# Graph attention on one core: the masks of query blocks 2 and 3 made between the first graph's steps instead of ahead of them

## The chip, the cores and the metric

The kernel runs on one core of a Trainium2 chip. A core has TensorE (PE: matrix products, results in PSUM), VectorE (DVE), ScalarE (ACT), GpSimd (POOL) and SyncE (SP, which here only starts DMAs), each with its own instruction queue that it works off in order. The metric is the device time of one launch in microseconds. The three runs shown for the kernel before gave 3195.69, 3188.96 and 3193.34 us, median 3193.34 us.

## The reference

There are 8 graphs of 2048 nodes with 256 channels, and one adjacency matrix that all graphs share. Each graph goes through 8-head masked attention (32 channels a head) and a small feed-forward block, with three layer norms:

```python
q, k, v = jnp.split(jnp.einsum('fnc,ck->fnk', x, w_qkv), 3, axis=-1)      # then split into 8 heads of 32
scores = jnp.einsum('fnhd,fmhd->fhnm', q, k) / jnp.sqrt(D)
scores = jnp.where((adj > 0)[None, None], scores, -1e9)
t = jnp.einsum('fhnm,fmhd->fnhd', jax.nn.softmax(scores, -1), v).reshape(F, N, C)
x = _layernorm(x + t, ln1_g, ln1_b)
h = jax.nn.relu(jnp.einsum('fnc,cd->fnd', x, w1) + b1)
x = _layernorm(x + jnp.einsum('fnd,dc->fnc', h, w2) + b2, ln2_g, ln2_b)
...
return _layernorm(x_in + x)      # the layer's own input added, normalised once more
```

`adj` is a 2048x2048 int32 matrix. A node attends where `adj > 0`.

## The kernel before

**Steps.** The work is cut into items `(f, qc, g, mb)`: graph `f` (8), query block `qc` of 512 queries (4), head group `g` of four heads (2), key block `mb` of 128 keys (16). That is 1024 items, 128 for a graph (a *frame*), and one pass of the main loop (line 606) is one step `t`. For an item, `scores` (line 222) forms four 128x512 score blocks on PE, keys on the partitions, and DVE adds the mask to them on their way from PSUM to a `p` tile (line 233, two instructions of 128x1024). `exponentials` is one ACT instruction of 128x2048 (line 237). `values` multiplies by V on PE and accumulates over the 16 key blocks in one PSUM bank (line 249). `add_up` sums the exponentials for the softmax denominator: some key blocks are added by POOL (line 271), six of 16 by a DMA that adds 1 MB in SBUF and that POOL issues (line 268). Scores run two steps ahead (`LEAD = 2`) and share three PSUM pairs, two per step.

**Fill.** All other work is written as generators and put between the steps by `advance` (line 511), once per step: projections of the next graph's keys and values (`project`), queries (`ask`), turning the next graph's input (`turn`), denominators, normalisation and feed-forward (`tail`). A generator that yields `BANK` asks for the one PSUM bank that is left for fill, and gets it at most once per step, if the step's credit (`STEP = 2200`, and `UNIT = 1024` at least) allows it or its due time has come. A positive number means: wait so many steps. `INPUTS - 2` means: wait until the two oldest of the three input buffers are free. `NEXT` (line 553) says at which step of a frame each piece for the next graph starts; `start` takes the due time as its last argument.

**Turning the input.** `turn` (line 169) loads 512 rows of the next graph's `x`, waits five steps, transposes them on PE in two bank uses (`turn_rows`, line 161), and stores the result in device memory as `XD`. `reload` fetches it again for the projections.

**Masks.** DVE adds an fp8 value of 0 or -57344 to a score. The mask depends only on `(qc, mb)`, so it is made once for all graphs. `begin` (line 557) does it ahead of the main loop for all four query blocks: for each 512x512 piece of `adj` (16 pieces, 1 MB each, 2 KB runs) it loads a `p` tile, DVE compares and converts to bf16 in two instructions (line 582), `mask_blocks` (line 134) transposes 16 blocks of 128x128 on PE (line 141), two PSUM banks of eight, and evicts one through ACT (line 147) and one through DVE (line 145) as one byte per element. SP stores each 128 KB half in device memory as `MD[qc, k]` (line 148). During query blocks 0 and 1, `begin` also turns the first graph's input and projects its keys and values. After the last piece of query block 1 it issues the first two items' scores and the first exponential (lines 598 to 601), and then goes on with query blocks 2 and 3. In the main loop `load_mask` (lines 607 and 608) fetches `MD` for the next query block, one piece at every odd step of the second head group, into a ring of nine mask tiles.

**Buffers that the change touches.** Keys and values live in rings of 11 tiles of 2 KB per partition (`kp`, `vp`, lines 71 and 73). `work` holds one tile each of `turned` and `hT` (4 KB), used by the tail of a query block, `yp` two tiles `y` (4 KB). The first tail of graph 0 starts at step 47.

Of the kernel before, what the change touches and what calls it, by code (L numbers as in the profile page):

```python
# [10 lines left out]
F32 = mybir.dt.float32  # L11
BF16 = mybir.dt.bfloat16
I32 = mybir.dt.int32
I8 = mybir.dt.int8
F8 = mybir.dt.float8e5
AF = mybir.ActivationFunctionType
ALU = mybir.AluOpType
AX = mybir.AxisListType

P = 128  # L20
H = 8
D = 32
CH = 512
# [6 lines left out]
BANK, MORE, WAIT, TURNED, ROOM, INPUTS = -1, -2, -3, -4, -5, -10  # L30
STEP, UNIT, TURN, KEPT = 2200, 1024, 1400, 2200

MASKED = -57344.0
CODE = -5.0
# [27 lines left out]
def fast_path(ctx, tc, cst, x, adj, out, RS):  # L62
    nc = tc.nc
    F, N, C = x.shape
    NCK, TPC, MB = N // CH, CH // P, N // P
# [5 lines left out]
    kp = ctx.enter_context(tc.tile_pool(name="kp", bufs=3 * NCK - 1))  # L71
    qp = ctx.enter_context(tc.tile_pool(name="qp", bufs=4))
    vp = ctx.enter_context(tc.tile_pool(name="vp", bufs=3 * NCK - 1))
    pp = ctx.enter_context(tc.tile_pool(name="pp", bufs=12))
    work = ctx.enter_context(tc.tile_pool(name="work", bufs=1))
    yp = ctx.enter_context(tc.tile_pool(name="yp", bufs=2))
# [8 lines left out]
    ident, identb, wqkv, w1s, w2s = cst["ident"], cst["identb"], cst["wqkv"], cst["w1s"], cst["w2s"]  # L85
    state = {"pair": 0, "side": None, "turn": 0, "turned": False, "holder": None, "tails": 0, "credit": 0}
# [15 lines left out]
    def bank(dt=F32):  # L102
        shape = [P, CH] if dt == F32 else [P, 2, CH]
        if state["side"] is not None:
            i = 1 - state["side"]
            return ps_x[i].tile(shape, dt, name=f"x{i}")
        i = state["turn"]
        state["turn"] = (i + 1) % 5
        pool = ps_s[i] if i < 3 else ps_x[i - 3]
        return pool.tile(shape, dt, name=f"s{i}" if i < 3 else f"x{i - 3}")  # L110
# [11 lines left out]


    MD = dp.tile([NCK, MB // 2, P, 2 * CH // 4], I32, name="md")
    MK = {}

    def words(mask):
        return mask.rearrange("p b q -> p (b q)").bitcast(I32)
# [5 lines left out]
    def mask_blocks(qc, mc, cv, to=None):  # L134
        for half in range(2):
# [11 lines left out]
                nc.scalar.copy(m.bitcast(I8), ps)  # L147
            nc.sync.dma_start(MD[qc, k], words(m))

    def load_mask(f, qc, k):  # L150
        nc.sync.dma_start(words(mask_piece(f, qc, k)), MD[qc, k])

# [16 lines left out]
    def turn(f, c):  # L169
        yield INPUTS - 2  # L170
        xc, xT = take([P, TPC, C], F32), take([P, 2, CH], F32)
        nc.sync.dma_start(xc, x[f, c * CH:(c + 1) * CH, :].rearrange("(j p) c -> p j c", p=P))
        yield 5
        yield from turn_rows(xc, xT)
        give(xc)
        yield 1
        nc.sync.dma_start(XD[f][c], xT)
        XT[f, c] = xT
        give(xT)
# [315 lines left out]
    def start(t, gen, due):  # L495
        fill.append([t, gen, 1, due])
        fill.sort(key=lambda e: e[3])
# [13 lines left out]
    def advance(t, finish=False):  # L511
        state["credit"] = min(max(state["credit"], 0) + STEP, KEPT)
        state["now"] = t
        free = not state["holder"]

        def more():
            if state["holder"] and state["holder"][2] == WAIT:
                return False
            due = [e[3] for e in fill if e[2] == BANK and e[0] <= t or e is state["holder"]]
            return finish or state["credit"] >= UNIT or min(due) <= t  # L520

        if state["holder"]:
            resume(state["holder"], t)
            while state["holder"] and more():
                resume(state["holder"], t)
        inputs = True
        for e in list(fill):
            while e[2] is not None and e[0] <= t and e is not state["holder"]:
                if e[2] == BANK:
                    if not free or not more():  # L530
                        break
                    free = False
                elif e[2] < INPUTS:
                    inputs = inputs and not any(u is not None for u in live[:INPUTS - e[2]])
                    if not inputs:
                        break
                elif e[2] == TURNED and state["turned"] or e[2] == ROOM and state["tails"] == 2:
                    break
                resume(e, t)
            while e is state["holder"] and more():  # L540
                resume(e, t)
# [3 lines left out]
    FRAME = 2 * NCK * MB  # L545


    def ask(f, c):
# [5 lines left out]
            60: [(project, 1, 0)], 66: [(ask, 3)], 72: [(turn, 3)], 80: [(project, 2, 0)], 98: [(ask, 0)], 100: [(project, 3, 0)],  # L554
            104: [(project, 0, 1)], 108: [(project, 1, 1)], 112: [(project, 2, 1)], 116: [(project, 3, 1)]}

    def begin():
        todo = deque((qc, c) for qc in range(NCK) for c in range(NCK))
        rows, cols = [], deque()

        def fetch():
            if todo:
                qc, c = todo.popleft()
                t = pp.tile([P, 4, CH], F32, name="p").bitcast(I32)
                nc.sync.dma_start(t, adj[qc * CH:(qc + 1) * CH, c * CH:(c + 1) * CH].rearrange("(j p) m -> p j m", p=P))
                cols.append((qc, c, t))

        for c in range(NCK):
            rows.append(pp.tile([P, 4, CH], F32, name="p"))
            xc = rows[c][:, 0:2, :].rearrange("p a (b c) -> p (a b) c", c=C)  # L570
            nc.sync.dma_start(xc, x[0, c * CH:(c + 1) * CH, :].rearrange("(j p) c -> p j c", p=P))
            fetch()
        fetch()
        while cols:
            qc, c, col = cols.popleft()
            if c % 2 == 0:
                two = pp.tile([P, 4, CH], F32, name="p").rearrange("p a q -> p (a q)").bitcast(BF16)
            cv = two[:, c % 2 * TPC * CH:(c % 2 + 1) * TPC * CH].rearrange("p (j m) -> p j m", m=CH)

            for half, what in enumerate((CODE, MASKED)):  # L580
                part = slice(half * 2 * P, (half + 1) * 2 * P)
                nc.vector.tensor_scalar(cv[:, :, part], col[:, :, part], 0.0, what, op0=ALU.is_le, op1=ALU.mult)
            fetch()
            xT = rows[c][:, 2:4, :]
            if qc == 0:
                yield from turn_rows(rows[c][:, 0:2, :].rearrange("p a (b c) -> p (a b) c", c=C), xT)
                nc.sync.dma_start(XD[0][c], xT)
                XT[0, c] = xT
                if c == 0:
                    yield from queries(0, 0, xT)  # L590
                yield from project(0, c, 0, xT)
            elif qc == 1:
                yield from project(0, c, 1, xT)
            if qc and c % 2 == 0:
                out4 = take([P, 4, 2, CH], F8)
                give(out4)
            yield from mask_blocks(qc, c, cv, [out4[:, c % 2 * 2 + i] for i in range(2)] if qc else None)
            if (qc, c) == (1, NCK - 1):
                for k in range(LEAD):
                    scores(items[k])  # L600
                exponentials(items[0])

    for _ in begin():
        pass
    state["side"] = 0
    for t, (f, qc, g, mb) in enumerate(items):
        if g == 1 and mb % 2 and (f + 1 < F or qc + 1 < NCK):
            load_mask(f + (qc + 1) // NCK, (qc + 1) % NCK, mb // 2)
        for what, *which in NEXT.get(t % FRAME, []):
            to = f if what is ask and which[0] else f + 1  # L610
            if to < F:
                at = (0, 0, 0) if what is turn else (which[0], 0, 0) if what is ask else (0, which[1], which[0] * TPC)
                start(t, what(to, *which), t + 3 * MB if what is turn else items.index((to, *at)) - LEAD - 1)
        if t == len(items) - MB // 2:
            xr, xb = state["rows"] = [take([P, TPC, C], F32) for _ in range(2)]
            nc.sync.dma_start(xr, x[f, qc * CH:(qc + 1) * CH, :].rearrange("(p j) c -> p j c", p=P))
        if t == len(items) - 2:
            nc.gpsimd.tensor_tensor(xb, xr, rows(cst["be2r"]), ALU.add)
        if t:
            advance(t)  # L620

        if t + 1 < len(items):
            exponentials(items[t + 1])
        if t + LEAD < len(items):
            nf, _, ng, nmb = items[t + LEAD]
            t0 = t
            while (nf, nmb // TPC, ng) not in V:
                advance(t0, finish=True)
                t0 += 1
            scores(items[t + LEAD])  # L630
        values(items[t])
        add_up(items[t])
        if mb == LAST and t + 1 < len(items):
            start(t + 2, denominator(f, qc, g, t + SUM), t + SUM + 4)
        if t == len(items) - 3:
            start(t, denominator(f, qc, g, t), t)
# [245 lines left out]
```

## Time and profile before

The profiled execution took 3196.28 us; the span from its first to its last instruction is 3194.5 us.

| what | value |
|---|---|
| profiled execution, its span | 3196.28 us, 3194.5 us |
| PE busy | 3081.7 us (96%) |
| DVE busy | 2749.6 us (86%) |
| POOL busy | 2593.3 us (81%) |
| ACT busy | 2417.7 us (76%) |
| mask add, line 233 | 2048 of 1218 ns |
| exponential, line 237 | 1024 of 1910 ns |
| adding DMAs, line 268 | 382 of 1 MB, 10.0 us from issue to landing |
| start of the 1st, 2nd and 3rd exponential | 62.5, 95.3, 101.1 us |
| main loop, second graph / third / fourth to seventh each | 391.7 / 379.4 / 381.2 us |

The last row is the time between the first exponentials of consecutive graphs. "Busy" is the time in which an engine had an instruction under way; PE's instructions overlap in a pipeline, so a busy PE need not be at its peak. A stretch of the span is read on its own: an engine's mean over the whole span says little about what sets the time there.

### The profile page before, as it was taken

To read this page: it belongs to the slowest core of one execution; us is meant where nothing else is said; L and a number is where in the kernel's file an instruction comes from. 1 tells how busy PE (TensorE), PEld (TensorE's weight loads), DVE (VectorE), ACT (ScalarE), POOL (GpSimd) and SP (SyncE) were. 2 spreads that over 40 slices of the span, in tenths; PEclk is the share of its full clock that TensorE was granted. 3 is DMA by queue.
4 is the path that set the end of the run, shared out by engine and by line. 5 is a ranking of instruction groups with operands and counts; after the bars stand their busy time and mean duration, and the time that the engine had idled before them with its cause. 6 is when DMAs were issued, how large, how long until landed. Compare 5 with 4: busy or idle time off the path is not lost. (4 is left out here: it accounts for less than half of the span.)

```text
span 3194.5 us, 68226 instructions
## 1 busy us (share of the span) xinstructions
PE 3081.7 (96%) x28868; PEld 963.0 (30%) x28868; DVE 2749.6 (86%) x3139; ACT 2417.7 (76%) x1909; POOL 2593.3 (81%) x1361
## 2 busy tenths in 40 slices
PE   7899999999999999999999999999999999999985
PEld 4222333222332223332333323323233233332222
DVE  4798988888889988889988988988988888889985
ACT  3677778777787777788777788778778778777774
POOL 0578888788888888888888888888889788889875
PEclk8899999999999999999999999999999999999998
DMA  9688889788798888898888899888879788888872
GB/s 323 142 192 193 183 175 199 161 188 189 179 195 188 191 194 178 176 204 196 187 177 174 194 208 198 168 182 196 196 174 203 177 196 192 176 177 166 178 150 64
DMA packets 153096, 589.46 MB, mean 185 GB/s; under 512 B 15024, under 2 KB 67760, under 8 KB 103888
## 3 DMA queue, kind: packets, MB, share of 16 engines
q0 software_dynamic: 64128, 433.22, 68.8%
q1 hardware_dynamic: 87840, 150.50, 13.7%
q8 instruction: 228, 3.74, 0.4%
q10 hardware_dynamic: 816, 1.31, 0.1%
q14 instruction: 84, 0.69, 0.1%
HBM read 146.67 MB, written 37.75 MB: 58 GB/s over the span
## 5 line engine op out<-in xcount | busy, mean ns | idle before, releaser
L233 DVE TENSOR_TENSOR p<-s,mask 128x1024 f32<-128x1024 f32 x2048 | 2409.1, 1218 | 325.0 <-PE s L230 182.9
L237 ACT ACTIVATE p<-p 128x2048 f32<-128x2048 f32 x1024 | 1956.0, 1910 | 566.5 <-DVE p L233 481.1
L271 POOL TENSOR_TENSOR p<-p 128x2048 f32<-128x2048 f32 x382 | 1875.4, 4909 | 359.1 <-ACT p L237 358.8
L230 PE MATMUL s<-qT,kT 32*128 32x512 f32 x8192 | 1172.5, 642 | 44.2 <-DVE p L233 39.4
L249 PE MATMUL x<-p,v 128*32 128x512 f32 x8192 | 1093.5, 606 | 4.6 <-ACT p L237 4.6
L230 PEld LDWEIGHTS s<-qT,kT 32*128 32x128 f32 x8192 | 320.9, 183 | 671.3 <-DVE p L233 643.6
L268 POOL DMA_DIRECT2D p<-p x382 | 416.8, 1092 | 70.1 <-ACT p L237 46.4
L249 PEld LDWEIGHTS x<-p,v 128*32 128x32 f32 x8192 | 161.5, 108 | 784.0 <-issue 310.2
L315 PE MATMUL x<-p,halves 128*32 128x512 f32 x2080 | 269.9, 595 | 0.0
L54 PE MATMUL x<-in,wqkv 128*32 128x512 f32 x1888 | 245.7, 592 | 0.0
L290 ACT ACTIVATE y<-y,nb,rs 128x256 f32<-128x256 f32 x372 | 219.1, 591 | 6.1 <-POOL nb L287 5.9
L278 DVE BATCH_NORM_STATS2 st<-y 128x6 f32<-128x256 f32 x372 | 155.0, 417 | 1.8 <-POOL y L370 1.8
L54 PE MATMUL x<-turned,w1s 128*32 128x512 f32 x992 | 123.9, 593 | 0.0
L54 PE MATMUL x<-w2s,hT 128*32 128x256 f32 x2016 | 121.8, 382 | 0.0
L54 PEld LDWEIGHTS x<-wqkv,in 128*32 128x32 f32 x3584 | 102.2, 110 | 64.1 <-issue 55.9
L54 PE MATMUL x<-wqkv,in 128*32 128x128 f32 x3584 | 117.4, 273 | 0.0
L315 PEld LDWEIGHTS x<-p,halves 128*32 128x32 f32 x2080 | 67.9, 111 | 156.9 <-issue 155.5
L368 POOL TENSOR_TENSOR y<-y,g2r 128x1024 f32<-128x1024 f32 x31 | 101.6, 3278 | 6.4 <-ACT y L290 6.4
L54 PEld LDWEIGHTS x<-in,wqkv 128*32 128x32 f32 x1888 | 61.3, 110 | 141.3 <-issue 116.5
L284 POOL TENSOR_TENSOR rs<-rs,mhalf 128x4 f32<-128x4 f32 x93 | 96.3, 1035 | 7.8
L370 POOL TENSOR_TENSOR y<-y,be2r 128x1024 f32<-128x1024 f32 x30 | 94.6, 3155 | 0.4
L54 PEld LDWEIGHTS x<-w2s,hT 128*32 128x32 f32 x2016 | 65.9, 111 | 70.7 <-issue 38.5
(121 smaller groups left out, 1301.1 us busy)
## 6 DMA issues: line engine op xcount, KB each, us to landing
p<-p POOLq DMA_DIRECT2D x382, 1024.0 KB, 10.0
in<-xd SPq DMA_DIRECT2D x87, 512.0 KB, 8.9
mask<-md SPq DMA_DIRECT2D x248, 128.0 KB, 8.6
y<-in_x_dram POOLq DMA_DIRECT2D x61, 512.0 KB, 10.1
p<-in_adj_dram SPq DMA_DIRECT2D x16, 1024.0 KB, 9.3
out_dram<-y SPq DMA_DIRECT2D x31, 512.0 KB, 6.2
in<-in_x_dram SPq DMA_DIRECT2D x30, 512.0 KB, 10.6
xd<-in SPq DMA_DIRECT2D x28, 512.0 KB, 8.8
```

What stands on the lines that cost most here:

```text
L54: nc.tensor.matmul(out[r:r + D], lhsT[:, r:r + D], rhs, start=start, stop=stop)
L230: nc.tensor.matmul(ps2[half][:, j, :], KT[f, mb // TPC, g][r:r + D, (mb % TPC) * P:(mb % TPC + 1) * P], QT[f, qc, g][r:r + D, :], start=Tr ...
L233: nc.vector.tensor_tensor(pt[:, 2 * half:2 * half + 2, :], ps, MK[f, qc, mb // 2][:, mb % 2, None, :].to_broadcast([P, 2, CH]), ALU.add)
L237: nc.scalar.activation(PT[item], PT[item], AF.Exp, scale=1.0 / math.sqrt(D))
L249: nc.tensor.matmul(O[grp][r:r + D, :], V[f, mb // TPC, g][:, mb % TPC, r:r + D], PT[item][:, h, :], start=(mb == 0), stop=(mb == LAST))
L268: nc.gpsimd.dma_start(PT[f, qc, g, chain[0]], PT.pop(item), accum_op=ALU.add)
L271: nc.gpsimd.tensor_tensor(first, first, PT.pop(item), ALU.add)
L278: nc.vector.bn_stats(st, t[:, j, :])
L284: nc.gpsimd.tensor_tensor(rs, rs, cst["mhalf"], ALU.pow)
L290: nc.scalar.activation(t[:, j, :], t[:, j, :], AF.Identity, bias=nb[:, j:j + 1], scale=rs[:, j:j + 1])
L315: nc.tensor.matmul(ps[r:r + D, :], cst["halves"][:, g, :], term[:, h, :], start=(n == 0), stop=(n == len(blocks) - 1))
L368: nc.gpsimd.tensor_tensor(z, z, rows(cst["g2r"]), ALU.mult)
```

## The change

`begin` makes the masks of query blocks 0 and 1 only. The masks of query blocks 2 and 3 are made by 16 jobs, `mask_job(n)`, that are started in the main loop at steps 2, 5, 8, ... 47. Each makes one `MD[qc, k]` (512 queries by 256 keys). A job takes one of four pairs of 2 KB parts, waiting a step at a time if none is free; SP loads two 512x128 pieces of `adj` into them (512-byte runs); five steps later ACT converts the first in place from int32 to bf16, one step later the second; then the job asks for the fill bank, PE transposes eight 128x128 blocks into it, and DVE compares, codes and evicts in one instruction of 128x1024 from PSUM to one byte, into the second half of the first part. One step later SP stores it, and three steps after that the pair can be used again.

The four pairs are borrowed: one K and one V tile (until step 128), `turned`, `hT` (each until step 41) and one `y` (until step 56). Since a K and a V tile are lent, six projections for the second graph start later in the first frame (`LATER`): the one at step 80 at 100, and the others by four steps each. `load_mask` first makes sure that its mask is `MADE`; if not, it runs fill without steps until it is. Lastly, `turn` waits seven steps instead of five, except when it loads the second graph's input (during the first frame).

```diff
+    def mask_job(n):
+        while not spare:
+            yield 1
+        parts, until = spare.popleft()
+        qc, k = divmod(n + MB, MB // 2)
+        for b, part in enumerate(parts):
+            nc.sync.dma_start(part.bitcast(I32).rearrange("p (j m) -> p j m", j=TPC),
+                              adj[qc * CH:(qc + 1) * CH, (2 * k + b) * P:(2 * k + b + 1) * P].rearrange("(j p) m -> p j m", p=P))
+        yield 5
+        cv = [part.bitcast(BF16)[:, 0:CH] for part in parts]
+        for b, part in enumerate(parts):
+            nc.scalar.copy(cv[b], part.bitcast(I32))
+            yield 1
+        yield BANK
+        ps = bank(BF16)
+        state["credit"] -= TURN
+        for b in range(2):
+            for j in range(TPC):
+                nc.tensor.transpose(ps[:, b, j * P:(j + 1) * P], cv[b][:, j * P:(j + 1) * P], identb)
+        m = parts[0][:, CH // 2:CH].bitcast(F8).rearrange("p (b q) -> p b q", b=2)
+        nc.vector.tensor_scalar(m.bitcast(I8), ps, 0.0, CODE, op0=ALU.is_le, op1=ALU.mult)
+        yield 1
+        nc.sync.dma_start(MD[qc, k], words(m))
+        MADE.add((qc, k))
+        yield 3
+        if state["now"] < until:
+            spare.append((parts, until))
...
-        yield 5
+        yield 5 if f == 1 else 7
         yield from turn_rows(xc, xT)
...
+    LATER = {80: [], 100: [(project, 2, 0)], 104: [(project, 3, 0)], 108: [(project, 0, 1)], 112: [(project, 1, 1)],
+             116: [(project, 2, 1)], 120: [(project, 3, 1)]}
...
-        todo = deque((qc, c) for qc in range(NCK) for c in range(NCK))
+        todo = deque((qc, c) for qc in range(2) for c in range(NCK))
...
+    n_mask = 0
+    spare.append(([kp.tile([P, CH], F32, name="kT"), vp.tile([P, TPC, P], F32, name="v").rearrange("p j c -> p (j c)")], FRAME))
+    for pool, name, until in ((work, "turned", 41), (work, "hT", 41), (yp, "y", 56)):
+        both = pool.tile([P, 2, CH], F32, name=name)
+        spare.append(([both[:, a, :] for a in range(2)], until))
     for t, (f, qc, g, mb) in enumerate(items):
         if g == 1 and mb % 2 and (f + 1 < F or qc + 1 < NCK):
+            t0 = t
+            while ((qc + 1) % NCK, mb // 2) not in MADE:
+                advance(t0, finish=True)
+                t0 += 1
             load_mask(f + (qc + 1) // NCK, (qc + 1) % NCK, mb // 2)
-        for what, *which in NEXT.get(t % FRAME, []):
+        while n_mask < MB and t >= 2 + 3 * n_mask:
+            start(t, mask_job(n_mask), 3 * MB - 2 + 2 * n_mask if n_mask < MB // 2 else 4 * MB - 2 + 2 * n_mask)
+            n_mask += 1
+        for what, *which in (NEXT if f else {**NEXT, **LATER}).get(t % FRAME, []):
```

More of the change, by code (lines that the diff above doesn't have):

```diff
@@ L124, in fast_path @@
     MD = dp.tile([NCK, MB // 2, P, 2 * CH // 4], I32, name="md")
-    MK = {}
+    MK, MADE, spare = {}, {(qc, k) for qc in range(2) for k in range(MB // 2)}, deque()
     def words(mask):
```

## The prediction

> **What bounds the kernel now.** First the page's slices (busy tenths of 40 slices of 80 us, then PE's granted clock):
>
> ```profile
> PE   7899999999999999999999999999999999999985
> PEclk8899999999999999999999999999999999999998
> ```
>
> PE is full in the main loop; only the ends, and a dip in the clock at the start, stand out. So I ask for stretches (us, then busy us and instruction count of PE, PEld, DVE, ACT, POOL; clock, DMA share, GB/s):
>
> ```profile
> 58.80:96.50 37.70, 18.33 (x144) 13.82 (x144) 24.12 (x28) 11.08 (x10) 0.00 (x0) 0.53 0.57 199
> 104.95:174.40 69.45, 63.97 (x504) 16.01 (x504) 61.23 (x52) 53.84 (x35) 54.82 (x22) 1.00 0.81 176
> 462.10:853.90 391.80, 381.86 (x3560) 117.89 (x3552) 338.60 (x384) 299.28 (x237) 324.63 (x169) 0.99 0.84 183
> 1233.20:1614.50 381.30, 379.31 (x3576) 117.19 (x3568) 338.05 (x384) 299.31 (x238) 324.92 (x169) 1.00 0.86 189
> ```
>
> Row 1 is the making of masks 2 and 3: PE half idle and at half clock. Row 3, the second graph, holds 10.5 us more than row 4, the fourth. The timeline inside row 1 (start, us, engine, line, what):
>
> ```profile
> 65.78 1.28 DVE L582 TENSOR_SCALAR p<-p 128x1024 bf16<-128x1024 int32 x2
> 66.52 1.03 PE L141 MATMUL s<-identb,p 128*128 128x128 bf16 x8 [3.08 <-DVE p L582]
> 67.59 1.01 ACT L147 CAST in<-s 128x1024 int8<-128x1024 bf16 x1 [3.17 <-PE s L141]
> 68.44 1.23 DVE L145 TENSOR_TENSOR in<-x,ones 128x1024 fp8e5<-128x1024 bf16 x1 [1.38 <-PE x L141]
> 69.58 1.28 DVE L582 TENSOR_SCALAR p<-p 128x1024 bf16<-128x1024 int32 x2
> ```
>
> The next piece starts 3.80 us later: convert, transpose, evict, one after the other, eight times. No step can hide it, since the second exponential stands behind it in ACT's queue.
>
> The second graph's excess, in the waits of PE (who waited for whom; total, times, longest) and its timeline:
>
> ```profile
> PE x L95 <- DMA in<-in_x_dram: 7.6, 2, 4.1
> 610.76 1.03 PE L95 MATMUL x<-ident,in 128*128 128x128 f32 x4 [4.06 <-DMA in<-in_x_dram]
> ```
>
> Twice (at 610.8 and 649.9) a turn's input came late; the clock records show half rate for 3.4 and 6.8 us right after or around it. Together that is the 10.5 us, 5.25 a stall.
>
> What a plain step costs, and one whose fill DVE evicts:
>
> ```profile
> 102.56 9.81 DVE L233 TENSOR_TENSOR p<-s,mask 128x1024 f32<-128x1024 f32 x8 [1.50 <-PE s L230]
> 199.17 2.35 DVE L233 TENSOR_TENSOR p<-s,mask 128x1024 f32<-128x1024 f32 x2
> 201.44 0.68 DVE L356 TENSOR_TENSOR y<-x,rc 128x512 f32<-128x512 f32 x1
> 202.04 2.34 DVE L233 TENSOR_TENSOR p<-s,mask 128x1024 f32<-128x1024 f32 x2
> 204.90 2.34 DVE L233 TENSOR_TENSOR p<-s,mask 128x1024 f32<-128x1024 f32 x2
> 207.51 2.36 DVE L233 TENSOR_TENSOR p<-s,mask 128x1024 f32<-128x1024 f32 x2 [0.27 <-PE s L230]
> ```
>
> Without fill a step is DVE's: 2.45 to 2.55 us, of which its pair takes 2.35 (PE needs 2.2: 1.14 scores and 1.06 values). A projection or denominator part takes 1.04 to 1.07 us of PE and makes the step PE's: 2.92. Four transposes with an ACT copy make 2.58 to 2.72. Here two steps with transposes and a DVE eviction took 2.87 and 2.86, and the projection step after them only 2.61 (204.90 to 207.51) instead of 2.92: what DVE adds is partly won back while PE is the longer one.
>
> **What the skill says.** (1) "VectorE: DVE Perf Modes", section "The TRN2 errata": from PSUM 120 cycles plus one per element at 0.96 GHz, so 1.21 us for 1024 by my estimate; the trace's 1.22 for the same shape (line 145) agrees. "What auto-detection actually checks" there asks for 16-bit tensors all round for the packed mode; the new eviction writes bytes, so I price it at 1.2 and keep 0.68 (what line 582 took from SBUF) as the low end. (2) Its ScalarE row, 224 cycles plus one per element at 1.2 GHz, gives 0.61 us for the new copies; the trace has 0.58 for 512 elements from PSUM (line 166). (3) "DMA: Bandwidth & Descriptors", "SWDGE vs HWDGE vs iDMA": each DMA engine goes round robin between the queues of SP's and of POOL's DMAs. The packet records agree: at 167 to 170 us every 0.65 us holds 16 of SP's 1 KB packets and 16 of the adding DMAs' 8 KB packets. (4) "TensorE: Matmul & The Clock Gate", "What's actually happening": an idle window of about 3.4 us halves PE's clock; the stalls of 4.06 and 3.49 us agree.
>
> **The change, part by part** (against the profiled span of 3194.5 us).
>
> *Masks 2 and 3 leave `begin`.* Before, the third exponential starts at 101.09, and its scores at 96.55, so 4.54 us from one to the other at half clock. After, these scores can start when DVE has freed the pair of item 1's first half, at about 64.75 (the adds of 63.51 run 2.36 for two). 64.75 + 4.54 = 69.3, so **-31.8 us**. The clock is half in both, so nothing is counted for it. The other DMAs and evictions removed lie inside this stretch and count no further.
>
> *Sixteen jobs come in.* DVE: one 1.2 us each, 19.5 in all. PE: eight transposes, 0.62 us at full clock (26.39 us: 8 in 0.62). In a step that was plain, DVE then needs 2.35 + 1.2 = 3.55, 1.0 more than 2.55: 16.0. Where a PE-bound fill step follows, up to 0.4 comes back (0.31 above); I count half of the jobs: -3.2. **+13 us.** Lower end: DVE idles 69.45 - 61.23 = 8.2 us in the second row, so 16 in the 135 us of these 48 steps; if all of it took the work, 19.5 - 16 = +3. Upper end: nothing won back and waits for the one bank, +20.
>
> *ACT's 32 copies* of 0.6: a step has 2.55 - 1.91 = 0.64 idle, before the next exponential's input. **0**; uncovered it would be 19 us. The copies stand ahead of an exponential in ACT's queue, so a late part holds exponential, values, PE.
>
> *SP:* 32 loads come in (eight of 1 MB go), and 16 stores move behind DVE's eviction. SP used to run ahead of the steps (the input issued at 179.9 is used at 247.4); now each store waits for DVE, and behind it are the next job's loads, reloads and mask loads. Mask loads lead by some 15 steps, reloads by 5: 0 if loads land. *DMA engines:* 1 KB packets take 46 ns, 4 KB ones 159, so 512 bytes about 27 by the line through both: 16384 x 27 / 16 = 28 us over 135 us, in which the share is 0.81. That is near 1.0. A job's load is issued about six steps before its first copy (after the store of the job three before it): 6 x 2.9 = 17.4 us. Nearest row: from 591.5 to 612.1 the SP queue moved 896 packets against adding DMAs, 43 per us; 1024 packets at that rate take 24 us, too long; but the adding queue pauses (145 to 155, 194 to 197, 232 to 243 us), and in pauses 1 KB packets ran at over 300 per us: 3 us. The first three jobs load before any adding DMA. I take one stall of 5.25: **+5 us**, from 0 to 16 x 5.25 = 84.
>
> *Lent tiles and `LATER`:* the same projections, 20 or four steps later, due from step 133 on: 0, -2 to +5 if they crowd. `MADE`: job k's mask is there about step 11 + 3k, wanted at 49 + 2k and 81 + 2(k-8): never waits.
>
> *Seven steps instead of five:* two steps of 2.9 are 5.8 us, more than the 4.06 and 3.49 missing. **-10.5 us**, 0 at worst if the late input only moves. Steps 2 later in other frames, which have no such wait: 0, within 5 either way.
>
> Sum: -31.8 + 13 + 5 - 10.5 = -24.3, so a span of 3170.2, 3172 for its execution. The median of the runs is 2.9 below the profiled execution: **3169 us**.
>
> **Rivals.** *A, late parts, slower:* SP's queue is served packet by packet against 8 KB adds, and ACT waits for most parts in the second and third query block's adds; each costs 5.25. Without the 5 I stand at -29; from six stalls the gain is gone, from seven it is slower by over 0.2%. Ten stalls: 3193 - 29 + 52 = 3216. For it: 24 us against 17.4; against: a stall stops the adding DMAs and so lets the queue empty. *B, some stalls:* four or five, -29 + 23 = 3187, on the border. *C, the longer wait wins nothing,* since the second graph's turns meet other traffic: 3169 + 10.5 = 3180. For it: one frame alone had the waits. *D, the change doesn't keep its place:* projections crowd after step 100 or fill runs without steps; some 25 us given back, 3194.
>
> **How the numbers follow.** Forecast 0.52 (own range 3158 to 3182), C 0.14, B 0.16, A 0.14, D 0.04. Within 0.2% (6.4 us, about what a measurement of this kernel can tell) is half of B and of D: 0.10. Faster 0.52 + 0.14 + 0.08 = 0.74, slower 0.14 + 0.02 = 0.16. Low end 3156: DVE's cost at +3 and no stall (-39) would be 3154. High end 3200: it takes in B, C, D and the mild end of A.
>
> **What would show it.** The third exponential near 69 us; steps with a mask eviction of 3.4 to 3.6 us; the evictions at 1.2 us; the second graph's frame near 381 with no wait of the turn's transposes on a DMA; frames three to seven within a us or two. It is wrong if ACT's copies wait for `adj` DMAs over and over with half clock after it (A), if the first frame grows by over 25 us, or if a turn's wait shows up in another frame.

## The result and the profile after

The changed kernel takes 3172.55 us (median of six runs, 3169.80 to 3174.60) against 3195.05 us (3188.96 to 3196.02) for the kernel before: ratio 0.9931, 95% interval 0.9920 to 0.9942, so 0.7% faster. The forecast was 3169 us. The profiled execution took 3173.02 us, its span 3171.2 us, 23.3 us less than before.

The first view is the page's slices of the changed kernel, to be laid beside those of before: the clock's 8s at the start are gone, and PE starts full one slice earlier.

```profile
PE   7999999999999999999999999999999999999985
PEclk9999999999999999999999999999999999999998
```

Where the 23.3 us are, from the starts of the exponentials in both traces:

| stretch | before | after | difference |
|---|---|---|---|
| start to 1st exponential | 62.5 | 64.1 | +1.6 |
| 1st to 4th exponential | 42.4 | 8.6 | -33.9 |
| rest of the first graph's frame | 357.2 | 371.5 | +14.4 |
| second frame | 391.7 | 383.3 | -8.4 |
| third frame | 379.4 | 381.4 | +2.0 |
| all that follows | 1961.3 | 1962.3 | +1.0 |

The timeline of the start (start, us, engine, line, operation) shows that the exponentials now follow each other at the pace of steps. In the kernel before, the second stood at 95.32 and the third at 101.09:

```profile
64.13 1.91 ACT L265 ACTIVATE p<-p 128x2048 f32<-128x2048 f32 x1 [4.37 <-DVE p L261]
66.61 1.91 ACT L265 ACTIVATE p<-p 128x2048 f32<-128x2048 f32 x1 [0.58 <-DVE p L261]
70.05 1.91 ACT L265 ACTIVATE p<-p 128x2048 f32<-128x2048 f32 x1 [1.53 <-DVE p L261]
```

A step with a mask eviction, from the timeline of the changed kernel. Line 261 is the mask add, line 168 the transposes of a job, line 170 its eviction:

```profile
98.09 2.35 DVE L261 TENSOR_TENSOR p<-s,mask 128x1024 f32<-128x1024 f32 x2
98.23 0.61 PE L168 MATMUL x<-identb,turned 128*128 128x128 bf16 x8
99.36 1.14 PE L258 MATMUL s<-qT,kT 32*128 32x512 f32 x8 [0.53 <-DVE p L261]
100.35 1.21 DVE L170 TENSOR_SCALAR turned<-x 128x1024 int8<-128x1024 bf16 x1
101.48 2.34 DVE L261 TENSOR_TENSOR p<-s,mask 128x1024 f32<-128x1024 f32 x2
```

From 98.09 to 101.48 are 3.39 us. DVE goes from the adds to the eviction to the next adds without a pause, and the 0.61 us of transposes lie beside it. So the step is DVE's. It is shorter than the 2.35 + 1.21 us of its instructions, since each starts about 0.09 us before the one ahead of it ends (100.35 against 98.09 + 2.35). Nearly all such steps in the first 64 are 3.39 or 3.40; one, which also holds statistics of a layer norm, is 4.03.

The new instructions' sizes, from the answers for their lines (duration in ns: least, median, most):

```profile
L170 DVE TENSOR_SCALAR turned<-x x3: 1211/1212/1214, 100.4 to 199.7; 128x1024 int8<-128x1024 bf16 x3
L161 ACT CAST turned<-turned x6: 602/604/621, 94.0 to 169.6; 128x512 bf16<-128x512 int32 x6
```

One stall is left in the first frame. The timeline at that place:

```profile
157.59 0.62 ACT L161 CAST kT<-kT 128x512 bf16<-128x512 int32 x1 [2.39 <-DMA kT<-in_adj_dram]
160.54 1.73 PE L277 MATMUL x<-p,v 128*32 128x512 f32 x8 [2.68 <-ACT oT L281]
165.32 2.36 DVE L261 TENSOR_TENSOR p<-s,mask 128x1024 f32<-128x1024 f32 x2 [4.19 <-PE s L258]
166.56 0.62 ACT L161 CAST turned<-turned 128x512 bf16<-128x512 int32 x1 [1.95 <-DMA turned<-in_adj_dram]
```

A part of `adj`, issued at 140.4, lands only at 157.6. ACT waits 2.39 us for it, with the exponential behind it; PE then waits for ACT; the clock records show half rate from 160.8 for 3.4 us, and DVE's adds come 6.54 us after the last ones, against 2.94 for the same step (34) of the kernel before. The stall is 3.6 us. In the 3.4 us ahead of the half rate (157.4 to 160.8) PE was busy for 0.72. The stretches around it (busy us of PE, PEld, DVE, ACT, POOL, then clock, DMA share, GB/s) show how full the DMA engines are there:

```profile
110.00:150.00 40.00, 35.15 (x292) 10.13 (x288) 36.89 (x33) 31.61 (x26) 26.32 (x11) 1.00 0.95 218
150.00:172.00 22.00, 18.55 (x144) 4.77 (x144) 16.14 (x15) 16.30 (x14) 8.87 (x4) 0.92 1.01 261
444.20:827.50 383.30, 380.90 (x3588) 117.71 (x3584) 338.32 (x384) 299.89 (x238) 325.67 (x169) 1.00 0.85 187
```

The last line is the second frame. Before it was 391.8 us with a clock of 0.99; now the clock is 1.00 and PE never waits for the input of a turn. Its DMA share of 0.85 is that of the later frames too; the 1.01 of the second line says that in the 22 us around the stall the engines were busy throughout.

### The profile page after: what moved, and what is told of

Its sections match the earlier page's. It is cut to its first block, busy times and chain, and to the rows that moved or that the text cites. A ratio compares the mean times of both kernels' runs of the same rounds, so it can differ in the third digit from the quotient of the medians.

```text
span 3171.2 us, 68285 instructions
## 1 busy us (share of the span) xinstructions
PE 3072.7 (97%) x28868; PEld 956.8 (30%) x28868; DVE 2746.2 (87%) x3131; ACT 2424.8 (76%) x1933; POOL 2592.9 (82%) x1361
## 5 line engine op out<-in xcount | busy, mean ns | idle before, releaser
L296 POOL DMA_DIRECT2D p<-p x382 | 411.8, 1079 | 68.7 <-ACT p L265 42.9
L54 PE MATMUL x<-turned,w1s 128*32 128x512 f32 (+1 forms) x1024 | 125.8, 586 | 0.8 <-ACT hT L451 0.6
L396 POOL TENSOR_TENSOR y<-y,g2r 128x1024 f32<-128x1024 f32 x31 | 101.1, 3260 | 6.4 <-ACT y L318 6.4
```

The costliest lines, as they stand in the source:

```text
L54: nc.tensor.matmul(out[r:r + D], lhsT[:, r:r + D], rhs, start=start, stop=stop)
L296: nc.gpsimd.dma_start(PT[f, qc, g, chain[0]], PT.pop(item), accum_op=ALU.add)
L396: nc.gpsimd.tensor_tensor(z, z, rows(cst["g2r"]), ALU.mult)
```

## Experiments

Each compares with the kernel before in the same session, whose median lay between 3192.87 and 3196.59 us. Differences of 2 us between sessions mean nothing. Frames are read from the exponentials of the profiled executions.

**1. Undo the longer wait.**

```diff
-        yield 5 if f == 1 else 7
+        yield 5
```

> The changed kernel with the turn's wait put back to five steps in all frames. If the longer wait is what took 8.4 us out of the second graph's frame (391.7 to 383.3 us), the two waits of the turn's transposes on their input come back there, with PE's half clock after them: frame near 391 to 394, time 3181 to 3183, some 9 to 10 us above the changed kernel. Rival: the waits went because the first frame's new order of DMAs shifted the second frame; then the frame stays near 383 and the time at 3172 to 3174.

Measured: 3173.67 us (3172.36 to 3173.98), ratio 0.9936 (0.9919 to 0.9952). The second frame is 383.3 us; the first seven frames are within 0.1 us of the changed kernel's, the last one within 0.3. In this kernel the longer wait does nothing. My theory's first half falls.

**2. The longer wait alone, on the kernel before.**

```diff
-        yield 5
+        yield 5 if f == 1 else 7
```

> The kernel before with the seven-step wait alone. If the wait is a cure by itself: second graph's frame 381 to 383 instead of 391.7, no wait on that DMA, time 10 us less, 3184 to 3186. If the late input only moves to another turn: another frame grows by 4 to 10 us and the time stays within 3 us of 3195. The third frame tells whether 379.4 against 381.4 us belongs to this wait.

Measured: 3186.67 us against 3195.97, ratio 0.9971 (0.9962 to 0.9979). Second frame 378.8 us, third 381.2, no wait on an input. By itself the wait is a cure, of some 9 us. The third frame's +1.8 comes with it.

**3. The later projections alone, on the kernel before** (`LATER` and its use, five steps of wait, no jobs).

```diff
+    LATER = {80: [], 100: [(project, 2, 0)], 104: [(project, 3, 0)], 108: [(project, 0, 1)], 112: [(project, 1, 1)],
+             116: [(project, 2, 1)], 120: [(project, 3, 1)]}
...
-        for what, *which in NEXT.get(t % FRAME, []):
+        for what, *which in (NEXT if f else {**NEXT, **LATER}).get(t % FRAME, []):
```

> The kernel before with the first frame's six later projections alone (wait of five steps, no jobs, no lent tiles). The second graph's two waits went away in the changed kernel without the longer wait too. If the later projections are what did that (they shift the second frame's fill towards the order of the later frames): second frame 381 to 384 instead of 391.7, no wait on the input, 8 to 10 us less, 3185 to 3187. If it was the jobs or the shorter start: waits stay, frame 391 to 394, time within 3 us of 3195.

Measured: 3186.64 us against 3196.59, ratio 0.9968 (0.9958 to 0.9979). Second frame 381.6 us, no wait, every later frame 381.2. So two edits of the change each cure the second frame, and the cure counts once. How, the timelines tell. In the kernel before, and with `LATER` alone, SP loads the third turn's input at about the same place, and it lands as late:

```profile
628.75 1.29 SPq L172 DMA_DIRECT2D in<-in_x_dram  x1
```

```profile
627.05 1.18 SPq L172 DMA_DIRECT2D in<-in_x_dram  x1
681.92 0.66 PE L95 MATMUL x<-ident,in 128*128 128x128 f32 x4
```

The first landed after 21.1 us, at 649.8, and PE stood waiting to use it (649.9). The second took 22.0 us, till 649.1, and is used at 681.9. For this turn the DMA isn't faster. The planner puts the transposes 13 steps later (step 201 instead of 188, counted by exponentials). From step 189 to 200 the fill bank goes, in all three kernels, to feed-forward, denominators and divisions, step by step. In the kernel before, the turn gets the last step ahead of them, 188. With `LATER` a projection has steps 187 and 188, and the turn comes after all of these. With seven steps of wait in the kernel before, it is the same: step 201. Two steps of wait thus move this turn by 13 steps, not two. The second turn's input, the other late one (610.8), is used at step 181 instead of 176 in both runs; there, with `LATER`, the load did land sooner too, 8.9 us after its issue instead of 18.8.

**4. No mask jobs.** The lent tiles and the later projections stay.

```diff
-            while ((qc + 1) % NCK, mb // 2) not in MADE:
-                advance(t0, finish=True)
-                t0 += 1
...
-        while n_mask < MB and t >= 2 + 3 * n_mask:
+        while False:
...
-        nc.sync.dma_start(words(mask_piece(f, qc, k)), MD[qc, k])
+        nc.sync.dma_start(words(mask_piece(f, qc, k)), MD[qc % 2, k])
```

> The changed kernel with the 16 mask jobs left out: query blocks 2 and 3 use the stored masks of blocks 0 and 1, so this part of the computation is missing and the answer is not the reference's. The lent tiles and the later projections stay. If the jobs cost what the steps show (16 evicting steps of 3.40 instead of about 2.6 to 2.9, and one stall of 3.6): first frame 14 us shorter than in the changed kernel, time 3157 to 3160. Rival: most of the first frame's extra 14 us is the projections' delay or other crowding, then only 3 to 6 us go and the time is 3167 to 3170.

Measured: 3154.62 us (3152.79 to 3156.01), ratio 0.9879 (0.9862 to 0.9895). The first frame is 365.3 us, 14.8 less than with jobs, the second 381.2, 2.1 less, so the jobs seem to push some work into the second frame. Less the stall of 3.6, a job costs (14.8 - 3.6) / 16 = 0.70 us of the first frame. Step by step, by the starts of DVE's adds, the 16 evicting steps are 13.3 us longer than the same steps without jobs, 0.83 each. The frames differ by less, among other things because in their first step, before any job evicts, the changed kernel was 0.9 us shorter in these two executions, and because a little comes back after the evicting steps. So a job costs 0.7 to 0.8 us. The rival, that the crowding is the cost, falls. In the 22 us from 150 on the DMA share is 0.85 without the jobs, against 1.01 with them.

**5. Nine steps for a job's loads.**

```diff
-        yield 5
+        yield 9
         cv = [part.bitcast(BF16)[:, 0:CH] for part in parts]
```

> The changed kernel with nine steps instead of five between a mask job's loads and its first copy. If the loads arrive late behind the adding DMAs (ACT's two waits of 2.4 and 1.9 us at 157 and 167 us and the half clock after them): both waits go, no step over 5 us in the first frame, time 3 to 4 us less, 3168 to 3170. Rival: ACT's wait was slack that PE and DVE would have had anyway, or jobs run late for lack of free pairs: 3172 to 3175.

Measured: 3205.19 us, ratio 1.0036 (1.0022 to 1.0051): slower than the kernel before. The stall at steps 31 to 34 is gone, but the first frame is 415.0 us, with 85.5 us for steps 80 to 95. The timeline there:

```profile
359.24 0.62 ACT L161 CAST kT<-kT 128x512 bf16<-128x512 int32 x1 [3.29 <-DMA kT<-in_adj_dram]
367.39 0.43 DVE L306 BATCH_NORM_STATS2 st<-y 128x6 f32<-128x256 f32 x1 [10.03 <-DMA y<-in_x_dram]
372.02 2.09 PE L258 MATMUL s<-qT,kT 32*128 32x512 f32 x8 [7.28 <-DVE p L261]
381.41 0.62 ACT L161 CAST kT<-kT 128x512 bf16<-128x512 int32 x1 [4.40 <-DMA kT<-in_adj_dram]
```

`turned`, `hT` and `y` are given back by then, the last jobs share the one pair of K and V, and their evictions come at steps 89, 91, 94 and 96, after `load_mask` has asked for them. The loop runs fill with no step between, and each load, each layer norm waits in the open. In the changed kernel the last eviction is at step 86 and the last mask is asked for at step 95: nine steps are all that keeps it from this.

**6. Seven steps for the loads, and one after the store,** so that the cycle of a pair stays.

```diff
-        yield 5
+        yield 7
         cv = [part.bitcast(BF16)[:, 0:CH] for part in parts]
...
         MADE.add((qc, k))
-        yield 3
+        yield 1
```

> The changed kernel with seven steps from a job's loads to its first copy and one step instead of three after the store, so that the cycle of a pair is as long as before. If the run with nine steps was slow only because the jobs ran out of pairs and steps ran fill alone for the missing masks, and late parts do cost a stall: no wait of the copies on their loads, no forced fill, first frame 3 to 4 us less, time 3168 to 3170. Rival: the stores' landing now holds SP and the parts are late again, 3172 to 3176, or masks are missing again, over 3180.

Measured: 3184.56 us, ratio 0.9970 (0.9957 to 0.9983), 12 us worse than the changed kernel. A copy still waits 3.7 us for its part, a step of 11.72 us stands at step 95, where the last eviction now is, and one of 8.38 at step 81, where PE waits for an input that SP fetched late:

```profile
PE x L54 <- DMA in<-xd: 4.0, 1, 4.0
```

So a part is late again and a mask is missing, as the rival had it; that the stores hold SP isn't shown. For the missing mask the trace has the reason: the pair of `y` serves three jobs here and four in the changed kernel, so after step 59 the pair of K and V has one job more to do, and the last job's loads go out at step 89 (335.8 us) instead of 76. Why a part was late with two steps more, this run doesn't say.

**7. Three steps for the loads.**

```diff
-        yield 5
+        yield 3
         cv = [part.bitcast(BF16)[:, 0:CH] for part in parts]
```

> The changed kernel with three steps instead of five between a job's loads and its first copy. If ACT waits for late parts and each wait goes through to the steps: the two waits grow by about 5.8 us each less what the stalled adding DMAs give back, two to five more appear, first frame 8 to 20 us longer, time 3180 to 3193. Rival: loads land by the pauses of the adding DMAs and waits are short: 3171 to 3176.

Measured: 3178.06 us (3175.96 to 3178.37), 5.5 above the changed kernel, less than I expected; first frame 384.8, 4.7 longer. The waits of ACT in the first frame:

```profile
ACT kT L161 <- DMA kT<-in_adj_dram: 6.7, 1, 6.7
ACT y L161 <- DMA y<-in_adj_dram: 2.3, 1, 2.3
```

With a third of 0.5 us they are 9.5 us against 4.3, but no flood of stalls. A pause of the adding DMAs follows: none is issued between 155.2 and 180.6 us, 25.4 us, where the changed kernel has 22.0 and the kernel without jobs 16.0. Loads issued in it, at 166 to 170 us, landed in 4 to 7 us. That the wait itself lengthens the pause fits these three numbers, but isn't shown apart.

**8. Halve the eviction.** ACT takes the first half of each (the same codes for entries of 0 and 1; `code` is a column of -5), DVE the second.

```diff
-        nc.vector.tensor_scalar(m.bitcast(I8), ps, 0.0, CODE, op0=ALU.is_le, op1=ALU.mult)
+        nc.scalar.activation(m[:, 0, :].bitcast(I8), ps[:, 0, :], AF.Identity, bias=cst["code"], scale=-CODE)
+        nc.vector.tensor_scalar(m[:, 1, :].bitcast(I8), ps[:, 1, :], 0.0, CODE, op0=ALU.is_le, op1=ALU.mult)
```

> The changed kernel with each job's eviction halved: ACT takes 128x512 of it (scale 5, bias -5, the same codes for entries of 0 and 1), DVE the other 128x512. If DVE's 1.21 us in one step is what makes the evicting steps 3.40: they fall to 2.85 to 2.95, the first frame by 7 to 9 us, time 3163.5 to 3166. Rival: PE's transposes or the one bank set those steps, or ACT becomes the bound (1.91 + 0.6 + 0.6 in a step): they stay over 3.2, time 3169 to 3174.

Measured: 3173.56 us (3172.38 to 3175.99), no gain. The evicting steps did fall, most of them to between 2.86 and 3.2 us, but the first frame is 381.6, since the stall took it back:

```profile
155.24 0.62 ACT L161 CAST y<-y 128x512 bf16<-128x512 int32 x1 [3.16 <-DMA y<-in_adj_dram]
160.99 0.62 ACT L161 CAST kT<-kT 128x512 bf16<-128x512 int32 x1 [5.13 <-DMA kT<-in_adj_dram]
```

The two steps around it take 12.35 and 3.71 us, against 3.40 and 6.54: 6.1 us lost here. The steps reach this place sooner, and the part lands no sooner (161.0, and 157.6 in the changed kernel). The 15 evicting steps outside the stall are 7.0 us longer than the same steps without jobs, against 12.5 in the changed kernel. So neither theory held whole: DVE sets the evicting steps, and the landing sets when the frame gets past step 33.

**9 and 10. The second load of each job on ACT's DMA queue,** with the whole and with the halved eviction.

```diff
-            nc.sync.dma_start(part.bitcast(I32).rearrange("p (j m) -> p j m", j=TPC),
+            (nc.scalar if b else nc.sync).dma_start(part.bitcast(I32).rearrange("p (j m) -> p j m", j=TPC),
```

> The changed kernel with the second load of each mask job issued on ACT's DMA queue instead of SP's. If parts are late because SP's one queue is served a packet for a packet of the adding DMAs, a second queue gives the pair twice the share: the slow landings (17.2 us at 140.4, 10 us at 156.4) fall to 6 to 12 us, ACT's two waits go, first frame 3 to 4 us less, time 3168 to 3170. Rival: the DMA engines as such are full and a second queue changes nothing, or issuing on ACT delays exponentials: 3172 to 3176.

> The halved eviction and the second load on ACT's DMA queue together. The halved eviction alone shortened the evicting steps from 3.40 to 2.86 to 3.2 us, but its one stall grew (a step of 12.35 us against 6.54), and the time stayed. If the stall was the landing of the parts, both gains now show: first frame 366 to 372 us instead of 380, time 3159 to 3165. If the DMA engines' total work sets that stretch, the stall stays and the time is 3170 to 3174.

Measured: 3180.04 us (ratio 0.9956, 0.9939 to 0.9972) and 3176.95 us (0.9944, 0.9928 to 0.9961), with first frames of 388.6 and 386.2 us, against 380.1 and 381.6 without the second queue. All times of run 9 lie above those of the changed kernel; for run 10, 3.4 us above run 8, they overlap. ACT's waits in the first frame of run 9:

```profile
ACT p L265 <- DMA kT<-in_adj_dram: 5.6, 1, 5.6
ACT p L265 <- DMA mask<-md: 4.4, 1, 4.4
ACT v L161 <- DMA v<-in_adj_dram: 2.8, 1, 2.8
```

Two are waits of exponentials: by the profile, a load issue just ahead of them in ACT's queue (119.65 and 159.18 us) waited for a DMA and held them. And landing is no better where it counts: the load of `v` on the second queue, issued at 146.5, took 24.4 us. So the run does not show more share for two queues; the new wait spoils it as a clean test of that.

**11 and 12. Half the packets.** Three of the four pairs become one part of 4 KB, loaded by one DMA in 1 KB runs; with the whole and with the halved eviction.

```diff
-        for b, part in enumerate(parts):
-            nc.sync.dma_start(part.bitcast(I32).rearrange("p (j m) -> p j m", j=TPC),
-                              adj[qc * CH:(qc + 1) * CH, (2 * k + b) * P:(2 * k + b + 1) * P].rearrange("(j p) m -> p j m", p=P))
+        width = 2 * P // len(parts)
+        for b, part in enumerate(parts):
+            at = 2 * k * P + b * width
+            nc.sync.dma_start(part.bitcast(I32).rearrange("p (j m) -> p j m", j=TPC),
+                              adj[qc * CH:(qc + 1) * CH, at:at + width].rearrange("(j p) m -> p j m", p=P))
...
-        spare.append(([both[:, a, :] for a in range(2)], until))
+        spare.append(([both.rearrange("p a q -> p (a q)")], until))
```

> The changed kernel with three of the four pairs (turned, hT, y) as one 4 KB part each, loaded by one DMA in 1 KB runs: same bytes, half the packets for 12 of 16 jobs, and two ACT copies as before. If a part is late because it moves a packet for each 8 KB packet of the adding DMAs, half the packets land in about half the time while those run: the step of 6.54 us goes to about 2.9, ACT's waits go, first frame 3 to 5 us less, time 3168 to 3170. Rival: the engines' time in bytes (46 against 2 times 27 ns, nearly the same) or the order of the queues' DMAs decides: waits stay, 3172 to 3175.

> The halved eviction with the 1 KB runs. If late parts are what took back the 6 to 7 us of the halved eviction, and half the packets land in time: evicting steps of 2.86 to 3.2, no step over 5 us, first frame 368 to 372 us instead of 381.6, time 3160 to 3164. If the landing is set by the adding DMAs' order and not by the count of packets: the stall near step 31 stays and the time is 3170 to 3174.

Measured: 3174.85 us (3173.52 to 3176.71) and 3169.22 us (3168.33 to 3170.12). In run 11 the wait moves to the pair that was left in two parts, and grows:

```profile
163.90 0.62 ACT L164 CAST v<-v 128x512 bf16<-128x512 int32 x1 [5.78 <-DMA v<-in_adj_dram]
```

That load was issued at 140.5, behind two others, and took 23.4 us; a wide one of 147.0 (512 KB), behind it in the queue, took 21.1. The load that is late still has its 512-byte packets, and only 10 of the 16 jobs came to use a wide part, so this is no clean test of the count. Run 12 still waits there, again for a part of the K and V pair (2.9 us the longest), with a first frame of 378.0. Its ratio to the kernel before, 0.9927 (0.9911 to 0.9944), can't be told from the changed kernel's 0.9931. Against run 11, in the same session, it is 5.6 us shorter, and the two sets of times don't overlap: here the halved eviction does gain. A stall somewhere in steps 29 to 35 stayed in every one of runs 8 to 12.

What the engines do there, the packet records of the changed kernel tell (packets, MB, share of the 16 engines' time). The first two lines are of the 4 us from 146, while adding DMAs run; the third is of the 2 us from 144, in which one of them ends, at 144.7. q0 is POOL's queue, q1 is SP's:

```profile
q0 software_dynamic: 99, 0.81, 97.2%
q1 hardware_dynamic: 122, 0.06, 7.1%
q1 hardware_dynamic: 977, 0.49, 84.1%
```

While an adding DMA runs, its 8 KB packets fill the engines, and SP's packets pass at about one for one, 30 a us. Around its end SP's queue moves some 490 a us. The late part of the changed kernel lands at 157.6, just after an adding DMA that ends at 157.2. So the engines are full there, and SP's queue gets its packets through in the gaps between adding DMAs. Whether halved packets for all pairs would end the stall wasn't run.

## Why the prediction was right, and where it was not

*Masks 2 and 3 leave `begin`, -31.8.* Right: the third exponential starts at 70.05, forecast 69.3, and the stretch up to it is 101.1 - 70.1 = 31.0 us shorter. The first exponential came 1.6 us later in this execution, whose clock records show half rate from 20.9 to 24.3 us, which those of before don't. The fourth gained another 1.2 us, since the clock was half for 3.4 us only, to 68.7: from the third to the fourth it took 2.65 us, but 3.93 or 3.94 in runs 5, 6 and 11, where the half rate lasted to between 70.5 and 72.0 us. I had counted nothing for the clock.

*Sixteen jobs, +13.* Right in mechanism and near in size: run 4 gives 0.7 to 0.8 us a job, 11 to 13 us, against 0.81. The evicting step was forecast at 3.55 from the sum and at 3.4 to 3.6 in the signs; it is 3.40, as the instructions overlap. So it costs 0.83 where I had 1.0, and some 1.4 us in all came back in the steps right after, where I had 3.2. Run 8 shows that DVE is what sets it: with half the eviction most fall to 2.86 to 3.2. The price of 1.2 us for the eviction was the right end: 1.21, so the packed mode did not engage for a byte output from PSUM, which is how I took it from the Trainium skill, "VectorE: DVE Perf Modes", section "What auto-detection actually checks". (The formula for PSUM in "The TRN2 errata" of the same page gives, as an estimate, 1.19 us for 1024 elements, where I wrote 1.21; the price I used was 1.2.)

*ACT's copies at nothing.* Right: 0.60 us each, and in the trace five exponentials waited for one, 3.1 us in sum. *DMA, +5.* One stall, as taken, of 3.6 us. The estimate of 27 ns for a 512-byte packet is what the packet records show at the median. The upper end, 16 stalls, was far off. Run 7 fits one reason, which I had given against rival A: the queue empties in the pause of the adding DMAs that a stall lengthens.

*Seven steps instead of five, -10.5.* This step failed. The second frame did lose 8.4 us and its waits, but run 1 takes the longer wait away and nothing comes back, and run 3 gets the cure from `LATER`, which I had priced at 0. I compared the 5.8 us of two steps with the missing 4.06 and 3.49, as if the waiting turn would stay where it was. What decides is where the planner places the turn in the fill, 13 steps on. That the frame came out shorter all the same was luck: another edit of the change, priced at nothing, has the same effect. Rival C said that the wait would win nothing, and was right in that, but wrong that the waits would remain: 3180 against 3172.55.

*`MADE`, "never waits".* It never waited, yet the reason I gave was wrong. I had job k's mask ready at about step 11 + 3k, so the last near 56; its eviction is at step 86, because the bank and the pairs are scarce: parts copied by step 32 get the bank at step 44, and after step 59 only the pair of K and V is left. Run 5 shows what lies nine steps further. Rival D had this mechanism, as fill run without steps, and gave 25 us back; in run 5 it gave back 33. Rivals A and B didn't come: there was one stall, not four or more.

*The sum.* -24.3 was forecast for the span, -23.3 measured; by stretch the misses are -0.5 up to the fourth exponential (-32.3 for -31.8), -3.6 in the rest of the first frame (14.4 for 18), +2.1 in the second frame and +3.0 after it. Of these 3.0 the third frame's 2.0 came in runs 2 and 3 as well (381.2 in both): its 379.4 was a feature of the kernel before, and I had not looked at that frame.

## What to carry to other kernels

Work at the head of a kernel, with one engine waiting for the next, gave back most of its length once it was spread over the steps of the main loop: 31.0 us up to the third exponential. What it costs there is read from the engine that gets one instruction more in its step, here 0.7 to 0.8 us for 1.21 us of VectorE. Where a planner orders the fill, an edit of timing can act by the new order and not by the time that it adds: try each such edit alone before crediting it. And buffers that are lent until a given step have a cliff behind that step: know how far the last user is from it.

## What the runs showed of the hardware

- While the adding DMAs run, a load of 256 KB on SP's queue took 17 to 23 us (140.4 to 157.6; 140.5 to 163.9 in run 11), and 3 to 4 us in their pauses (165.3 to 168.5). In the 4 us from 146 it got 122 packets of 512 bytes through beside 99 of 8 KB. A load on ACT's queue (24.4 us in run 9) and one of 512 KB in 1 KB runs (21.1 us in run 11) were as slow there.
- Two steps less between load and copy, some 5.8 us for each of 16 jobs, raised the sum of ACT's waits for parts only from 4.3 to 9.5 us, and the time by 5.5 us (run 7).
- PE's clock went to half rate for 3.4 us after 3.4 us in which PE was busy for 0.72 (157.4 to 160.8).
- VectorE started an instruction about 0.09 us before the one ahead of it had ended (100.35 against 100.44).
- VectorE's compare-and-code from PSUM, bf16 to one byte, 128x1024: 1.21 us, the same as the 1.22 of the two-input form. ScalarE in place from int32 to bf16, 128x512: 0.60 us, with the output over the input's first half.
